# Two chained attention layers in 32-bit floats: layer 1's softmax without a maximum for seven of eight images, and a split load of the weights

## The chip, the core and the metric

The kernel runs on one core of a Trainium2 chip. The core has five engines that run side by side, each with its own queue of instructions: TensorE (PE, matrix products; PEld is its loading of the stationary operand), VectorE (DVE), ScalarE (ACT), GpSimd (POOL) and SyncE (SP), which in this kernel issues the DMAs. Matrix products are written to PSUM, which is used here in banks of 128 x 512 floats, and DVE and ACT carry them from there to SBUF. The metric is the device time of one execution in microseconds (us); lower is better.

## The reference

There are 8 images of 32 x 32 positions, so N = 1024 tokens, with C = 256 channels. Layer 0 is self-attention with 4 heads of width 256, an output projection and a residual. Layer 1 is a gated self-attention with keys of width 32. Cut to what matters:

```python
# layer 0
qkv = einsum('bnc,cd->bnd', x, W_qkv)            # 4 heads, q, k, v of 256 each
q, k, v = split(qkv.reshape(B, N, 4, 768), 3, axis=-1)
atten = softmax(einsum('bihd,bjhd->bijh', q, k) * 256 ** -0.5, axis=2)
res = einsum('bijh,bjhd->bihd', atten, v).reshape(B, N, 1024)
x = einsum('bnd,dc->bnc', res, W_out) + b_out + x
# layer 1
f, g, h = x @ Wf + bf, x @ Wg + bg, x @ Wh + bh  # widths 32, 32, 256
s = einsum('bik,bjk->bij', g, f)
o = einsum('bij,bjd->bid', softmax(s, axis=-1), h)
x = gamma * o + x
```

## The kernel before

**Layer 0** is cut into steps: one for each image, head and half of the queries (a block of 512). Weights are folded once at the start: `fold_weights(h)` turns the query, key and value weights of a head by PE (`pwq`, `pwk`, `pwv`, L293) and multiplies them to `wqk` and `wvo` (L309). After that a head needs the transposed image `x0T`, the products `q` of it with `wqk`, scores, exponentials, weighted sums `y` of the rows and a projection by `wvo` (`po`, L628), which is scaled by an inverse sum and added to the residual (L639). The three large products (queries, scores, weighted sums) are made from seven block products in place of eight. `seven` holds the recipe (its matmuls are L237, its additions L254), and DVE makes the sums of blocks that it needs: `sums` (L571) for the exponentials, `key_sums` (L396) for `x0T`, `value_sums` (L412) for the rows.

Layer 0's softmax takes no maximum. The sums of the exponentials go through DVE, an all-reduce on POOL (L584) and two small DMAs into columns, and their reciprocals are kept in `inverse` (L597). At the very end `judge` counts on DVE and POOL how many of the kept reciprocals lie within bounds, `decide` turns this into a flag, and if one does not, a branch runs everything again in a general form with maxima (`General0` and `Layer1`).

**Layer 1** of image b - 1 is a unit of two steps (`Layer1`). It stands between heads 1 and 2 of image b, for b = 7 behind the four heads; layer 1 of the last image (`final`) comes after all steps. `scores` makes eight products of 128 keys by 512 queries into eight PSUM banks (`ps_l`, L735), and ACT copies them to `s_l` (L744). `Softmax.have` takes maxima over the keys on DVE (L781, L785, L787) and over the partitions on POOL (L789). `pieces` subtracts the maximum on DVE (L796) and takes the exponential on ACT (L801), in four parts each. `row_products` then multiplies by the values, which carry a column of ones (`pa_l`, L814), takes the reciprocal of the sum (L822, into a small tile `r`) and adds the scaled product to the residual (L824).

**The order.** On PE, DVE and ACT the order is written out by hand: each step collects tasks with `put(tasks, *at)`, where `at` is a place within the step, and emits them sorted by place. An engine runs its queue in that order, so that an instruction that waits holds up all behind it. DMAs on SP and the work of POOL are placed by the framework. Six PSUM banks (`ps`) go round among scores, weighted sums and layer 1's products, and two others (`psm`) among the rest. A product that takes a bank waits until the bank's last reader is done.

The transposed image of the next image is made in two parts. 32 DMAs per image move blocks of 32 x 32 (`x0T<-x`, L368), and four DVE transposes (`squares`, L373) turn what lies within the blocks. The latter are placed at 0.4, 1.4, 2.4 and 4.4 of the step of head 3, block 0, of images 0 to 6.

**The start.** The first image is loaded, its blocks are transposed by PE (`px`, L341), and ACT copies them out (L344). `load_weights` issues two DMAs per head: all of its columns of `W_qkv` as one (L187) and its rows of `W_out` (L188). The biases and layer 1's weights follow (`load_rest`), then the next image.

Of the kernel before, what the change touches and what calls it, by code (L numbers as in the profile page):

```python
# [10 lines left out]
F32 = mybir.dt.float32  # L11
AF = mybir.ActivationFunctionType
# [8 lines left out]
def kernel(  # L21
# [63 lines left out]
    CV = C + 4  # L85
    SCALE = C ** (-0.5)
    SUM_LOW, SUM_HIGH = N / 8.0, N * 8.0


    x_v = x.rearrange("b h w c -> b (h w) c").rearrange("b (k p t) c -> b p k (t c)", p=P, t=HT)  # L90
# [60 lines left out]
    bh_sb = const.tile([P, C], F32, tag="bh", name="bh_sb")  # L151
    gamma_sb = const.tile([P, 1], F32, tag="gamma", name="gamma_sb")

    inverse = const.tile([P, B * HEADS * NBLK * HT], F32, tag="inverse", name="inverse")

    def load_rest():
# [24 lines left out]
    def load_weights(h, tag):  # L181

        nw = CC * 3 * C
        t = tile_of(tag, [P, nw + CC * C], f"w_{h}")
        w = t[:, :nw].rearrange("p (c d) -> p c d", c=CC)
        wo = t[:, nw:].rearrange("p (c d) -> p c d", c=CC)
        nc.sync.dma_start(w, wqkv_v[:, :, ts(h, 3 * C)])  # L187
        nc.sync.dma_start(wo, wout_v[:, ts(h, CC), :])  # L188
        weights[h] = w, wo

# [455 lines left out]
    class Layer1:  # L646
        scale = 1.0

        def __init__(self, b):
            self.b, self.name = b, f"{b}_l1"  # L650
            self.s = {}
            self.fg = None

# [71 lines left out]
        def scores(self, blk):  # L725

            n = f"{self.name}_{blk}"
            four = P // CK
            soft = Softmax(self, blk)

            def task(j0):
                pms = []
                for r in range(four):
                    pm = tile_of("ps", [P, NB], f"ps_{n}_{j0 + r}")
                    nc.tensor.matmul(  # L735
                        pm,
                        lhsT=self.f[ts(r, CK), ts(j0 + r, P)],
                        rhs=self.g[ts(r, CK), ts(blk, NB)],
                        start=True,
                        stop=True,  # L740
                    )
                    pms.append(pm)
                for r, pm in enumerate(pms):
                    nc.scalar.copy(soft.tile()[:, j0 + r, :], pm)  # L744

            have = [
                partial(soft.have, [(j0, j0 + 2), (j0 + 2, j0 + four)])
                for j0 in range(0, NT, four)
            ]
            return [partial(task, j0) for j0 in range(0, NT, four)], have + soft.pieces()  # L750

        def products(self, blk):
            return row_products(self, blk, rows1)
# [53 lines left out]
    def row_products(a, blk, acc_rows):  # L807


        def task(ti):  # L810
            p, v = a.s[blk], a.v
            pm = tile_of("ps", [P, NB], f"pa_{a.name}_{blk}_{ti}")
            for j in range(NT):
                nc.tensor.matmul(  # L814
                    pm[:, : C + 1],
                    lhsT=p[:, j, ts(ti, P)],
                    rhs=v[:, j, : C + 1],
                    start=(j == 0),
                    stop=(j == NT - 1),
                )  # L820
            r = tile_of("r", [P, 1], f"r_{a.name}_{blk}_{ti}")
            nc.vector.reciprocal(r, pm[:, C : C + 1])  # L822
            acc = acc_rows[a.b][:, blk * HT + ti, :]
            nc.vector.scalar_tensor_tensor(acc, pm[:, :C], r, acc, ALU.mult, ALU.add)  # L824
            a.done(blk, ti)

        return [partial(task, ti) for ti in range(HT)]
# [43 lines left out]
    for b in range(B):  # L871
        units = [Layer0(b, h) for h in range(HEADS)]
        if b > 0:
            units.insert(behind(b), Layer1(b - 1))
        steps += [(u, blk) for u in units for blk in range(NBLK)]
    final = Layer1(B - 1)

# [18 lines left out]
    for i, (a, blk) in enumerate(steps):  # L896
        l0 = isinstance(a, Layer0)
        one, two, nxt = step(i - 1), step(i - 2), step(i + 1)
        places = []

        def put(tasks, *at):
            assert len(tasks) == len(at)
            places.extend(zip(at, range(len(places), len(places) + len(at)), tasks))

        if l0:
            put(a.scores(blk), 0, 2, 4, 6, 8, 10)
        else:
            tasks, pieces = a.scores(blk)
            put(tasks, *((0.5, 2.4) if blk == 0 else (0.5, 2)))
            put(pieces, *((1.6, 3.9, 6.2, 6.5, 7.4, 8.4, 8.6) if blk == 0 else  # L910
                          (0.9, 2.7, 4.2, 5, 6.2, 6.8, 7.5)))
        if is_l0(two):
            u, k = two
            put(u.products_of[k][2:], 1 if l0 else 0)
            put([partial(u.invert, k)], 2.9 if l0 or blk == 1 else 1.9)
            put(u.project(k), *((3, 7) if l0 else (2, 6) if blk == 0 else (3, 7)))
        if is_l0(one):
            u, k = one
            sums, keys = u.sums(k)
            u.products_of[k] = u.products(k)  # L920
            put(sums[:2] + sums[3:], *((2.2, 3.2, 4.2) if l0 else (0.8, 2.2, 4.5)))
            put(sums[2:3], 5.2 if l0 else 5.5)
            put(keys, *((6.2, 8.2) if l0 else (7.6, 9.6)))
            put(u.products_of[k][:2], *((5, 9) if l0 else (4, 7)))
        elif one is not None:
            put(one[0].products(one[1]), *((3, 5, 7, 9) if l0 else (1, 4, 6, 8)))
        if i == 0:
            put(fold[2:], -2, -1, *[1.5 + 0.6 * n for n in range(len(fold) - 4)])
            put(first_sums[:2], 8.4, 9.4)
        if i == 1:  # L930
            put(first_sums[2:], 1.4, 3.4)
            put([partial(nc.vector.tensor_scalar, bh_sb, bh_sb, gamma_sb, None, ALU.mult)], 8.5)

        if is_l0(nxt) and blk == NBLK - 1:
            queries, qsums = nxt[0].queries()
            put(queries, *((2.5, 4.5, 6.5) if not l0 else
                            (1.5, 2.5, 4.5) if is_l0(two) else (0.5, 2.5, 5.5)))
            put(qsums, *((6.7, 6.9, 7.3, 7.6) if not l0 else
                          (5.4, 6.4, 7.2, 7.4) if is_l0(two) else (6.4, 7.2, 7.3, 7.4)))

        if l0 and a.h == 0 and blk == 0:
            put(residual(a.b), 5.3, 6.3, 7.3, 7.4)
        if l0 and a.h == 0 and blk == 1 and a.b > 0:
            put(value_sums(a.b), 1.4, 2.4, 3.4, 4.4)
        if l0 and a.h == 2 and blk == 0 and a.b + 1 < B:
            load_x(a.b + 1)
        if l0 and a.h == 2 and blk == 1 and a.b + 1 < B:
            moves, squares = turn_rows(a.b + 1, rows, xT_of, 0)
            put(moves, *range(1, 9))
        if l0 and a.h == HEADS - 1 and blk == 0 and a.b + 1 < B:  # L950
            put(squares, 0.4, 1.4, 2.4, 4.4)
            put(key_sums(a.b + 1), 5.4, 6.4, 7.2, 7.4)

        if l0 and a.b > 0 and a.h == behind(a.b) - 1:
            if blk == 0:
                moves, turned = turn_rows(a.b - 1, rows1, x1T_of, 1, step(i + 2)[0].fg_tile)
                put(moves, 0.1, 0.2, 0.3, 0.4)
                put(turned, 5.4, 6.4, 7.2, 7.4)
            else:
                tasks, moves = nxt[0].queries_apart()  # L960
                put(tasks, 1.5)
                put(moves, 1.6, 1.7, 1.8, 1.9)
        if not l0 and blk == 0:
            put(a.values(), 0.9, 1, 3, 5, 8)
        if nxt is None:
            put(transpose_rows(B - 1, rows1, x1T_of, 1), 8.1, 8.2, 8.3, 8.4)
            put(final.queries(), 9, 9.1, 9.3)
        for _, _, t in sorted(places, key=lambda x: x[:2]):
            t()


    count = const.tile([P, 1], F32, tag="count", name="count")
    total = const.tile([P, 1], F32, tag="total", name="total")
    flag = const.tile([P, 1], mybir.dt.int32, tag="flag", name="flag")

    def judge():
        n = inverse.shape[1]
        good = tile_of("rs", [P, n], "good")
        nc.vector.tensor_scalar(good, inverse, 1.0 / SUM_HIGH, None, ALU.is_ge)
        nc.vector.scalar_tensor_tensor(good, inverse, 1.0 / SUM_LOW, good, ALU.is_le, ALU.mult)  # L980
        nc.vector.tensor_reduce(count, good, op=ALU.add, axis=AX.X)
        nc.gpsimd.partition_all_reduce(total, count, P, bass_isa.ReduceOp.add)

    def decide():
        n = inverse.shape[1]
        nc.vector.tensor_scalar(flag, total, P * n - 0.5, None, ALU.is_lt)

    (s0, p0), (s1, p1) = final.scores(0), final.scores(1)
# [9 lines left out]
    class General0:  # L998
# [31 lines left out]
        def scores(self, blk):  # L1030
# [15 lines left out]

            return [partial(task, j0) for j0 in range(0, NT, 4)], soft.pieces()

        def done(self, blk, ti):
            pass  # L1050

# [54 lines left out]
```

## Time and profile before

| what | value |
|---|---|
| three runs: median (lowest to highest) | 2349.11 us (2348.98 to 2349.63) |
| the profiled execution: its time, its span | 2347.16 us, 2345.4 us |
| TensorE clock granted, mean | 1.000 |
| layer 1's subtraction, DVE L796 | 64 of 1217 ns |
| layer 1's maxima, DVE L781, L785, L787 | 32 of 1218, 16 of 1226, 16 of 692 ns |
| layer 1's exponential, ACT L801 | 64 of 1059 ns |
| layer 1's copy out of PSUM, ACT L744 | 128 of 600 ns |
| layer 1's maximum over partitions, POOL L789 | 16 of 1783 ns |

The page of the profile tells of one execution. The span runs from the first instruction to the last. Busy times count when at least one instruction of an engine is under way; on PE the ends of matmuls are modelled, and neighbours overlap. A line of the waits has the waiting engine, tile and line, what it waited for, and then the total in us, how often, and the longest. A line of the timeline has start, duration, engine, line, operation, output<-input, shapes and a count where equal instructions that follow each other are merged; a bracket at its end gives the idle time before it and what ended it. Line numbers are those of the kernel before.

### The profile page before, as it was taken

To read this page: it belongs to the slowest core of one execution; us is meant where nothing else is said; L and a number is where in the kernel's file an instruction comes from. 1 tells how busy PE (TensorE), PEld (TensorE's weight loads), DVE (VectorE), ACT (ScalarE), POOL (GpSimd) and SP (SyncE) were. 2 spreads that over 40 slices of the span, in tenths; PEclk is the share of its full clock that TensorE was granted. 3 is DMA by queue.
4 is the path that set the end of the run, shared out by engine and by line. 5 is a ranking of instruction groups with operands and counts; after the bars stand their busy time and mean duration, and the time that the engine had idled before them with its cause. 6 is when DMAs were issued, how large, how long until landed. Compare 5 with 4: busy or idle time off the path is not lost.

```text
span 2345.4 us, 26265 instructions
## 1 busy us (share of the span) xinstructions
PE 2329.4 (99%) x10394; PEld 1917.0 (82%) x10394; DVE 1606.1 (68%) x2506; ACT 580.0 (25%) x931; POOL 236.5 (10%) x93
## 2 busy tenths in 40 slices
PE   9999999999999999999999999999999999999999
PEld 6888888788878888788887888878888788888877
DVE  6667776577775767757777577675776757766665
ACT  2222222222232222322223222232222322222232
POOL 0111110011110111101111011110011101101110
PEclk9999999999999999999999999999999999999999
DMA  4000010100101001110011000110001100000100
GB/s 137 1 1 1 1 37 15 33 1 8 29 17 32 1 19 21 19 28 1 19 26 18 24 1 19 30 18 19 1 19 30 19 19 1 1 1 1 30 10 29
DMA packets 169172, 42.96 MB, mean 18 GB/s; under 512 B 158097, under 2 KB 161937, under 8 KB 169041
## 3 DMA queue, kind: packets, MB, share of 16 engines
q1 hardware_dynamic: 169040, 41.20, 7.9%
q8 instruction: 84, 1.38, 0.2%
q14 instruction: 48, 0.39, 0.1%
HBM read 13.37 MB, written 8.52 MB: 9 GB/s over the span
## 4 chain that ended last, share of the span: by engine, by line
PE 95%; DVE 4%; DMA 0%; ACT 0%; issue 0%; SPq 0%; DVEq 0%; ACTq 0%
PE psy L237 14%; PE psy_y L237 14%; PE psx L237 9%; PE pa_l L814 9%; PE psz L237 9%; PE po L628 9%; PE psx_y L237 9%; PE psz_y L237 9%; PE psy_q L237 4%; PE psx_q L237 2%; PE psz_q L237 2%; PE pr_v_l L457 2%; PE ps_l L735 1%; DVE s_l L796 1%; PE pm_fg L693 1%; DVE s L571 0%
## 5 line engine op out<-in xcount | busy, mean ns | idle before, releaser
L584 POOL PARTITION_ALL_REDUCE rb<-rs x64 | 206.9, 3233 | 1880.6 <-DVE rs L582 1880.6
L532 ACT ACTIVATE p<-p 128x1024 f32<-128x1024 f32 x128 | 135.3, 1057 | 562.1 <-DVE p L254 562.1
L237 PE MATMUL psx<-q,x0T 128*128 128x256 f32 x1024 | 263.5, 380 | 0.0
L237 PE MATMUL psy<-qs,xs 128*128 128x256 f32 x1024 | 262.9, 379 | 0.0
L237 PE MATMUL psz<-q,xs 128*128 128x256 f32 x1024 | 262.8, 379 | 0.0
L237 PE MATMUL psy_y<-s,xt 128*128 128x256 f32 x1024 | 243.0, 380 | 2.6 <-DVE s L571 2.4
L628 PE MATMUL po<-wvo,y 128*128 128x256 f32 x1024 | 242.0, 379 | 0.0
L237 PE MATMUL psx_y<-p,x 128*128 128x256 f32 x1024 | 241.9, 379 | 0.0
L814 PE MATMUL pa_l<-v_l,s_l 128*128 128x257 f32 x1024 | 231.7, 381 | 2.3 <-DVE y L254 1.9
L237 PEld LDWEIGHTS psx<-q,x0T 128*128 128x128 f32 x1024 | 193.9, 190 | 45.4 <-issue 20.7
L628 PEld LDWEIGHTS po<-wvo,y 128*128 128x128 f32 x1024 | 194.5, 190 | 40.0 <-issue 15.1
L814 PEld LDWEIGHTS pa_l<-v_l,s_l 128*128 128x128 f32 x1024 | 193.7, 190 | 39.0 <-issue 12.7
L237 PEld LDWEIGHTS psx_y<-p,x 128*128 128x128 f32 x1024 | 194.6, 190 | 34.1 <-issue 8.6
L237 PEld LDWEIGHTS psy_y<-s,xt 128*128 128x128 f32 x1024 | 191.6, 190 | 35.4 <-PE psx_y L237 5.0
L237 PEld LDWEIGHTS psy<-qs,xs 128*128 128x128 f32 x1024 | 194.5, 190 | 26.8 <-DVE qs L503 0.4
L237 PEld LDWEIGHTS psz<-q,xs 128*128 128x128 f32 x1024 | 194.6, 190 | 26.4
L254 DVE TENSOR_TENSOR u<-psy,e 128x512 f32<-128x512 f32 x128 | 88.5, 692 | 146.1 <-ACT e L260 73.5
L266 ACT ACTIVATE p<-psx 128x512 f32<-128x512 f32 x128 | 76.4, 597 | 409.8 <-PE psx L237 409.6
L254 DVE TENSOR_TENSOR v<-psy,e 128x512 f32<-128x512 f32 x128 | 88.0, 688 | 125.1 <-PE psy L237 125.1
L237 PE MATMUL psy<-qs,x0T 128*128 128x256 f32 x512 | 131.5, 379 | 0.8 <-DVE v L254 0.8
L639 DVE SCALAR_TENSOR_TENSOR x<-po,inverse,x 128x256 f32<-128x256 f32 x256 | 112.0, 479 | 16.9 <-PE po L628 6.6
L260 ACT COPY e<-psx 128x512 f32<-128x512 f32 x128 | 73.8, 577 | 201.4 <-PE psx L237 201.4
(116 smaller groups left out, 3056.7 us busy)
## 6 DMA issues: line engine op xcount, KB each, us to landing
out_dram<-x SPq DMA_DIRECT2D x15, 512.0 KB, 2.6
x<-in_x_dram SPq DMA_DIRECT2D x14, 512.0 KB, 4.8
x0T<-x SPq DMA_DIRECT2D x224, 32.0 KB, 1.9
fg<-x SPq DMA_DIRECT2D x112, 64.0 KB, 2.3
fg<-fg SPq DMA_DIRECT2D x56, 64.0 KB, 2.0
w<-in_L_conv_W_qkv_dram SPq DMA_DIRECT2D x4, 768.0 KB
x<-in_x_dram SPq DMA_DIRECT2D x4, 256.0 KB, 4.4
w<-in_L_conv_W_out_dram SPq DMA_DIRECT2D x4, 256.0 KB, 9.8
```

Of the source, the lines that this page charges most:

```text
L237: nc.tensor.matmul(banks[k][:, ts(i, w)], lhsT=lhsT, rhs=rhs, start=first and n == 0, stop=True, skip_group_check=True,)
L254: nc.vector.tensor_tensor(dst, shaped(banks[k]), shaped(other), ALU.add)
L260: nc.scalar.copy(scratch("e"), banks["x"])
L266: copy(outs["11"](), shaped(banks["x"]))
L457: nc.tensor.matmul(pm[:, ts(j, C)], lhsT=src()[:, c, ts(2 * t2 + j, P)], rhs=w()[:, c, :], start=(c == 0), stop=(c == CC - 1),)
L532: exp(both, both)
L584: nc.gpsimd.partition_all_reduce(t, r.rearrange("p e i -> p (e i)"), P, bass_isa.ReduceOp.add)
L628: nc.tensor.matmul(pm[:, ts(j, C)], lhsT=self.y[blk][:, c, ts(2 * t2 + j, P)], rhs=folded[self.h][1][:, c, :], start=(c == 0), stop=(c == ...
L639: nc.vector.scalar_tensor_tensor(acc, pm[:, ts(j, C)], inverse[:, n : n + 1], acc, ALU.mult, ALU.add)
L693: nc.tensor.matmul(pm[ts(k, half)], lhsT=w[:, c, :], rhs=x1T_of[b][:, c, ts(k, NB)], start=(c == 0), stop=(c == CC - 1),)
L735: nc.tensor.matmul(pm, lhsT=self.f[ts(r, CK), ts(j0 + r, P)], rhs=self.g[ts(r, CK), ts(blk, NB)], start=True, stop=True,)
L814: nc.tensor.matmul(pm[:, : C + 1], lhsT=p[:, j, ts(ti, P)], rhs=v[:, j, : C + 1], start=(j == 0), stop=(j == NT - 1),)
```

## The change

Four things are changed.

- For the first seven images, layer 1 takes the exponential directly when it carries the scores out of PSUM (`direct=True`). The maxima, their all-reduce, the subtraction and the later exponential are left out. The last image keeps them.
- The reciprocals of these images' sums are kept in a constant `inverse1` of 56 columns, and `judge` counts them too, within 2^-64 and 2^64, adding both counts.
- The third of the four transposes of `x0T` moves from place 2.4 to 3.4 of its step.
- `load_weights` splits the load of `W_qkv`: queries' and keys' columns first, then the values' columns.

```diff
         w = t[:, :nw].rearrange("p (c d) -> p c d", c=CC)
         wo = t[:, nw:].rearrange("p (c d) -> p c d", c=CC)
-        nc.sync.dma_start(w, wqkv_v[:, :, ts(h, 3 * C)])
+        for part in (slice(0, 2 * C), slice(2 * C, 3 * C)):
+            nc.sync.dma_start(w[:, :, part], wqkv_v[:, :, ts(h, 3 * C)][:, :, part])
         nc.sync.dma_start(wo, wout_v[:, ts(h, CC), :])
...
+            exp = partial(nc.scalar.activation, func=AF.Exp, scale=self.scale)
...
                 for r, pm in enumerate(pms):
-                    nc.scalar.copy(soft.tile()[:, j0 + r, :], pm)
-
+                    (exp if self.direct else nc.scalar.copy)(soft.tile()[:, j0 + r, :], pm)
+
+            tasks = [partial(task, j0) for j0 in range(0, NT, four)]
+            if self.direct:
+                return tasks, []
...
+        def inverse_of(self, blk, ti):
+            if self.direct:
+                n = (self.b * NBLK + blk) * HT + ti
+                return inverse1[:, n : n + 1]
+            return tile_of("r", [P, 1], f"r_{self.name}_{blk}_{ti}")
...
-            r = tile_of("r", [P, 1], f"r_{a.name}_{blk}_{ti}")
+            r = a.inverse_of(blk, ti)
...
-            units.insert(behind(b), Layer1(b - 1))
+            units.insert(behind(b), Layer1(b - 1, direct=True))
...
-            tasks, pieces = a.scores(blk)
+            tasks, _ = a.scores(blk)
             put(tasks, *((0.5, 2.4) if blk == 0 else (0.5, 2)))
-            put(pieces, *((1.6, 3.9, 6.2, 6.5, 7.4, 8.4, 8.6) if blk == 0 else
-                          (0.9, 2.7, 4.2, 5, 6.2, 6.8, 7.5)))
...
-            put(squares, 0.4, 1.4, 2.4, 4.4)
+            put(squares, 0.4, 1.4, 3.4, 4.4)
...
     def judge():
-        n = inverse.shape[1]
-        good = tile_of("rs", [P, n], "good")
-        nc.vector.tensor_scalar(good, inverse, 1.0 / SUM_HIGH, None, ALU.is_ge)
-        nc.vector.scalar_tensor_tensor(good, inverse, 1.0 / SUM_LOW, good, ALU.is_le, ALU.mult)
-        nc.vector.tensor_reduce(count, good, op=ALU.add, axis=AX.X)
+        for k, (inv, low, high) in enumerate(
+            ((inverse, SUM_LOW, SUM_HIGH), (inverse1, 1.0 / FAR, FAR))
+        ):
+            good = tile_of("rs", [P, inv.shape[1]], f"good{k}")
+            nc.vector.tensor_scalar(good, inv, 1.0 / high, None, ALU.is_ge)
+            nc.vector.scalar_tensor_tensor(good, inv, 1.0 / low, good, ALU.is_le, ALU.mult)
+            nc.vector.tensor_reduce(counts[:, k : k + 1], good, op=ALU.add, axis=AX.X)
+        nc.vector.tensor_tensor(count, counts[:, 0:1], counts[:, 1:2], ALU.add)
         nc.gpsimd.partition_all_reduce(total, count, P, bass_isa.ReduceOp.add)
```

More of the change, by code (lines that the diff above doesn't have):

```diff
@@ L87 @@
     SUM_LOW, SUM_HIGH = N / 8.0, N * 8.0
+    FAR = 2.0**64
     x_v = x.rearrange("b h w c -> b (h w) c").rearrange("b (k p t) c -> b p k (t c)", p=P, t=HT)
@@ L152 @@
     gamma_sb = const.tile([P, 1], F32, tag="gamma", name="gamma_sb")
+    inverse1 = const.tile([P, (B - 1) * NBLK * HT], F32, tag="inverse1", name="inverse1")
     inverse = const.tile([P, B * HEADS * NBLK * HT], F32, tag="inverse", name="inverse")
@@ L647, with __init__ @@
         scale = 1.0
-        def __init__(self, b):
-            self.b, self.name = b, f"{b}_l1"
+        def __init__(self, b, direct=False):
+            self.b, self.name, self.direct = b, f"{b}_l1", direct
             self.s = {}
@@ L749, in scores @@
             ]
-            return [partial(task, j0) for j0 in range(0, NT, four)], have + soft.pieces()
+            return tasks, have + soft.pieces()
+        def inverse_of(self, blk, ti):
[3 more added lines that the diff above has]
+            return tile_of("r", [P, 1], f"r_{self.name}_{blk}_{ti}")
         def products(self, blk):
@@ L972 @@
     count = const.tile([P, 1], F32, tag="count", name="count")
+    counts = const.tile([P, 2], F32, tag="counts", name="counts")
     total = const.tile([P, 1], F32, tag="total", name="total")
@@ L976, in judge @@
     def judge():
-        n = inverse.shape[1]
-        good = tile_of("rs", [P, n], "good")
-        nc.vector.tensor_scalar(good, inverse, 1.0 / SUM_HIGH, None, ALU.is_ge)
-        nc.vector.scalar_tensor_tensor(good, inverse, 1.0 / SUM_LOW, good, ALU.is_le, ALU.mult)
-        nc.vector.tensor_reduce(count, good, op=ALU.add, axis=AX.X)
+        for k, (inv, low, high) in enumerate(
[6 more added lines that the diff above has]
+        nc.vector.tensor_tensor(count, counts[:, 0:1], counts[:, 1:2], ALU.add)
         nc.gpsimd.partition_all_reduce(total, count, P, bass_isa.ReduceOp.add)
     def decide():
-        n = inverse.shape[1]
+        n = inverse.shape[1] + inverse1.shape[1]
         nc.vector.tensor_scalar(flag, total, P * n - 0.5, None, ALU.is_lt)
@@ L1047, in scores, with inverse_of @@
             return [partial(task, j0) for j0 in range(0, NT, 4)], soft.pieces()
+        def inverse_of(self, blk, ti):
+            return tile_of("r", [P, 1], f"r_{self.name}_{blk}_{ti}")
         def done(self, blk, ti):
```

## The prediction

> **What bounds the kernel now.** I read the page first, then the waits of TensorE (PE), then the timeline around each place where PE waits. From the page's head and its table of engines:
>
> ```profile
> span 2345.4 us, 26265 instructions
> ...
> PE 2329.4 (99%) x10394; PEld 1917.0 (82%) x10394; DVE 1606.1 (68%) x2506; ACT 580.0 (25%) x931; POOL 236.5 (10%) x93
> ```
>
> PE is the bound from end to end, and every other engine has a third of the span or more to spare. Work taken off DVE, ACT and POOL is worth only what it takes out of PE's waits. These are the waits of PE (total, times, longest) that bear on the change:
>
> ```profile
> PE psy_y L237 <- DVE s L571: 2.4, 7, 0.3
> PE pa_l L814 <- DVE y L254: 1.9, 7, 0.3
> PE pwq L293 <- DMA w<-in_L_conv_W_qkv_dram: 1.1, 1, 1.1
> ```
>
> They are few, and understated: matmuls overlap, so a wait counts as idle only once the one before has drained. I therefore measure from start to start. The timeline shows 8 matmuls of 256 columns in 1.89 us, with 0.38 us for one, so the pitch is (1.89 - 0.38) / 7 = 0.216 us. The first wait, in the period of image 2:
>
> ```profile
> 498.43 0.70 DVE L373 STREAM_TRANSPOSE x0T<-x0T 128x512 f32<-128x512 f32 x1
> 499.06 0.14 DVE L597 RECIPROCAL inverse<-st 128x4 f32<-128x4 f32 x1
> 499.21 1.89 PE L237 MATMUL psx_y<-p,x 128*128 128x256 f32 x8
> 499.30 0.88 DVE L639 SCALAR_TENSOR_TENSOR x<-po,inverse,x 128x256 f32<-128x256 f32 x2
> 500.09 1.22 DVE L571 TENSOR_TENSOR s<-ss,p 128x1024 f32<-128x1024 f32 x1
> 501.45 0.45 PE L237 MATMUL psy_y<-s,xt 128*128 128x256 f32 x1 [0.34 <-DVE s L571]
> ```
>
> `psy_y` was due at 499.21 + 8 x 0.216 = 500.94 and began at 501.45, 0.14 us after `s` was ready (500.09 + 1.22 = 501.31): 0.51 us lost. Its eight then took 1.97 us in place of 1.89, 0.08 more. So 0.58 us, once per image for images 0 to 6. Ahead of `s` stands one transpose that has no hurry.
>
> The second wait, in layer 1's second block:
>
> ```profile
> 407.62 1.22 DVE L796 TENSOR_TENSOR s_l<-s_l,cmax_l 128x1024 f32<-128x1024 f32 x1
> 408.75 0.69 DVE L581 TENSOR_TENSOR rs<-m 128x512 f32<-128x512 f32 x1
> 408.96 1.14 PE L735 MATMUL ps_l<-fg 32*128 32x512 f32 x8
> 409.81 0.42 DVE L254 TENSOR_TENSOR y<-psy_y,e_y 128x256 f32<-128x256 f32 x1
> 410.38 0.46 PE L814 MATMUL pa_l<-v_l,s_l 128*128 128x257 f32 x1 [0.27 <-DVE y L254]
> ```
>
> From the start of `ps_l` to the next work PE takes 1.42 us here. At the three other groups of `ps_l` in this layer (384, 389 and 414 us) it is 1.07. `pa_l` gets a PSUM bank that `y<-psy_y` empties, ready at 410.23, although PE had filled it by 407.4: DVE stood in the subtraction of the maximum. Loss 0.35 us, less 0.03 for the slower restart that the other groups show, so 0.32, again 7 times.
>
> **What the skill says.** "Perfetto Trace Analysis", Identifying the Most-Contended Engine, calls matmul busy time a poor measure because matmuls are pipelined. The trace agrees: weight loads fill 82% where PE shows 99%, and the 0.51 us above show as 0.34. "ScalarE: Activation LUTs", Step-by-step: what each stage is for, says that throughput is the same for every function. It agrees: exponentials out of PSUM (128x512) take 597 ns, layer 1's copies 600. "DMA: Bandwidth & Descriptors", Anatomy of one DMA (told there for GpSimd's path; these loads are SyncE's), says that the semaphore fires only after the last byte is confirmed. Here the last 3,072-byte packet of head 0's weights ends at 8.15 us and PE starts on them at 9.20. "TensorE: Matmul & The Clock Gate", Part 1: The HAM clock gate, says PE starts throttled until it has been busy for a while. It agrees: 128-column transposes have a pitch of 0.216 us up to 7.7 and 0.110 from 9.2.
>
> **The change, part by part.**
>
> *No maximum in 14 of layer 1's 16 blocks.* Per block it removes on DVE 2 x 1.218 + 1.226 + 0.692 + 4 x 1.217 = 9.2 us (rows L781, L785, L787, L796), on ACT 4 x 1.059 = 4.2 us (L801), on POOL 1.78 us (L789). Over 14 blocks that is 129, 59 and 25 us. The copy becomes an exponential, 600 against 597 ns: nothing, and banks come free as before. None of this is on the path but for the second wait. There the last subtraction ahead of `y<-psy_y` goes, and so do the three before it. DVE's `v_l`, `rs`, `rs` and `y` then follow their inputs, and `y<-psy_y` is done near 408, two microseconds before the bank is wanted at about 410.0. Gain 7 x 0.32 = 2.2 us. PE's own order is the same in both programs, instruction for instruction.
>
> *One transpose from 2.4 to 3.4.* DVE's order shows it directly behind `s`. The reciprocal and everything up to `s` move up by its 0.63 us (499.06 - 498.43): `s` ends at 500.68, PE may go at 500.82, and it is due at 500.94. The wait closes with 0.12 us to spare. The reciprocal's own input was issued at 492.05 and such a copy lands about 2 us later; `po` is there at 497.7. The transpose then ends at 501.3, where `p<-psy` (501.22) begins as before, and its reader, a key sum, starts at 505.61. Gain 7 x 0.58 = 4.1 us; without the restart 3.6.
>
> *Queries' and keys' weights first.* SP issues four more DMAs at about 0.45 us each; the bytes are the same. What queues behind them on SP are the biases, the next image's load (22.2 us) and its moves (29.4), whose product is first read near 200: hidden. Head 1's weights are wanted at 18.9 and their last packet ends at 10.75: hidden. Head 0's first two thirds arrive earlier: the 171st of 256 packets of 3,072 bytes ends at 7.05, so 1.1 us sooner. From the timeline of the start:
>
> ```profile
> 8.17 0.58 ACT L344 COPY x0T<-px 128x512 f32<-128x512 f32 x1 [0.27 <-PE px L341]
> ...
> 9.20 0.63 PE L293 MATMUL pwq<-ident,w 128*128 128x128 f32 x4 [1.07 <-DMA w<-in_L_conv_W_qkv_dram]
> 9.67 0.27 PE L293 MATMUL pwk<-ident,w 128*128 128x128 f32 x1
> ```
>
> `pwq` may then start near 8.1, at the slow pitch (4 x 0.216), and `pwk` near 8.9, since its bank is empty at 8.17 + 0.58 = 8.75. That is 0.8 us before 9.67. `pwv` newly waits for its own DMA, whose bytes were all there at about 9.1, and is due at about 9.8. All later waits of the start are chains between engines that move along. Bounds: 0 (the third copy gates) to 1.2 us; I take 0.8.
>
> *The judgement.* Three small DVE operations and one addition more. Nothing in the trace is this narrow and of this kind but reciprocals (166 ns); I bound them by 0.6 and 1.2 us in all (256-wide ones take 282 to 424 ns). DVE sat idle 0.99 us before the reciprocal that follows (at 2329.91), and PE waits for neither: nothing. Writing the reciprocals into a wider constant costs nothing.
>
> Sum: 4.1 + 2.2 + 0.8 = 7.1 us from a span of 2345.4. The runs' median is 2349.11, the profiled one's time 2347.16: launch and end lie outside the span and are not touched. 2349.1 - 7.1 = 2342.0, -0.30%. What a measurement of this kernel can tell from no change is about 0.2%, 4.7 us.
>
> **Rivals.** *The transposition closes nothing*, because `s` still comes a tenth late or another instruction takes the hole. For it: the margin is only 0.12 us. Against: even then most of 0.51 goes. Time: 2349.1 - 3.0 = 2346.1. *The bank wait stays*, with another holder of the bank: 2349.1 - 4.9 = 2344.2. Against it: DVE's end and PE's start are 0.15 us apart, as at the first wait. *The start gives nothing*: 2342.8, inside the forecast. *DVE's relief helps more than the two waits*: the remaining losses in the middle (0.18 us at `psy_y` once an image, changes between 32-row and full matmuls) lie where no removed instruction stands, so at most 7 x 0.26 = 1.8 more, 2340.2.
>
> *Slower: the judgement fails and the general path runs behind the fast one.* Place: the branch after the last product. It decides from a row sum outside 2^64 either way, 44.4 in logarithm. Price, estimated from the trace's pitches (256 columns 0.216, 512 columns 0.429, two passes each): a head needs 6.9 for queries, 6.9 for values, 27.5 for scores, 27.8 for products, so 276 us for four, and layer 1 some 35: 8 x 311 = 2490, in all 4835 us. Against it: worked out from the reference's inputs, the logarithms of layer 1's row sums lie between 10.9 and 33.6. Otherwise the change only takes work from queues whose order stays; the three things that it adds are the DMAs, the moved transpose and the judgement, all with slack above.
>
> **Chances.** Forecast (the start's rival with it) 0.76; bank wait stays 0.08, half of which still passes 0.2%; transposition closes nothing 0.12; more gain 0.02; slower 0.02. Faster 0.76 + 0.04 + 0.02 = 0.82, within 0.2% 0.04 + 0.12 = 0.16, slower 0.02. Range: low 2341.0 (all gains at their upper bound, 7.5, and the runs' spread of 0.6), high 2345.0, which takes in the bank rival and half closings of the first wait.
>
> **What would show it.** Right: both waits gone from PE's list, `s` ending 0.1 us or more before `psy_y` is due, 1.07 us from `ps_l` to `pa_l`, `pwk` near 8.9, DVE busy near 1477 us with PE's pitch unchanged. Wrong: a new releaser in front of `psy_y` or `pa_l`, PE waiting for a later weights copy, or a second pass over all images.

## The result, and the profile after

The changed kernel takes 2341.31 us (median of 6 runs, 2340.5 to 2343.82); the kernel before, beside it, 2349.05 (6 runs, 2347.45 to 2349.63). The ratio is 0.997, with an interval from 0.9957 to 0.9983: 4.0 to 10.1 us shorter. The forecast was 2342.0.

The head of the page of the changed kernel, its table of engines and the shares of the chain that ended last (line numbers in a view are those of its own kernel, from here on):

```profile
span 2341.0 us, 26029 instructions
...
PE 2329.5 (100%) x10394; PEld 1918.5 (82%) x10394; DVE 1482.5 (63%) x2398; ACT 522.8 (22%) x875; POOL 211.6 (9%) x79
...
PE 99%; DVE 1%; DMA 0%; ACT 0%; SPq 0%; issue 0%; ACTq 0%
```

PE does the same work in a span that is 4.4 us shorter. DVE lost 123.6 us of busy time, ACT 57.2 and POOL 24.9. The waits of PE in the changed kernel (total, times, longest):

```profile
PE px L344 <- DMA x<-in_x_dram: 1.9, 3, 1.4
PE pm_idle L873 <- DVE col L133: 1.1, 1, 1.1
PE psy L240 <- DVE v L257: 0.8, 1, 0.8
PE pwk L296 <- ACT wvo L176: 0.8, 1, 0.8
PE pwv L296 <- ACT wqT L176: 0.7, 1, 0.7
PE pa_l L828 <- DVE v_l L723: 0.4, 1, 0.4
```

Both lines with seven waits, `psy_y` for `s` and `pa_l` for `y`, are gone, and so is `pwq` for its DMA. What is left stands once or three times. The first line is in the start, where PE waits for the image, and it is longer than before:

```profile
PE px L341 <- DMA x<-in_x_dram: 0.6, 2, 0.4
```

I cut the span at two marks that every version has: the first matmul of the first `psy_y`, and the last matmul of the last `pa_l` (start to start, so that modelled ends play no part).

| | before | after | difference |
|---|---|---|---|
| start of the span to the first `psy_y` | 62.74 us | 64.66 us | +1.92 |
| first `psy_y` to the last `pa_l` ("the middle") | 2277.15 us | 2270.85 us | -6.30 |
| last `pa_l` to the end | 5.5 us | 5.5 us | 0 |

So the middle is 6.3 us shorter, and the start of this one execution is 1.9 us longer.

The timeline of the changed kernel in the period of image 2, where `psy_y` waited (start, duration, then what ran):

```profile
499.44 0.17 DVE L600 RECIPROCAL inverse<-st 128x4 f32<-128x4 f32 x1
499.72 0.88 DVE L642 SCALAR_TENSOR_TENSOR x<-po,inverse,x 128x256 f32<-128x256 f32 x2
500.23 1.89 PE L240 MATMUL psx_y<-p,x 128*128 128x256 f32 x8
500.51 1.22 DVE L574 TENSOR_TENSOR s<-ss,p 128x1024 f32<-128x1024 f32 x1
501.64 0.70 DVE L376 STREAM_TRANSPOSE x0T<-x0T 128x512 f32<-128x512 f32 x1
501.95 1.89 PE L240 MATMUL psy_y<-s,xt 128*128 128x256 f32 x8
```

The transpose now stands behind `s`. `psy_y` is due at 500.23 + 8 x 0.216 = 501.96 and starts at 501.95; all eight form one row of 1.89 us. `s` ends at 501.73, 0.22 us before; of that PE needs the usual 0.14 from DVE's end to its own start, so 0.08 us was to spare.

The place of the second wait in the changed kernel:

```profile
408.53 0.42 DVE L585 TENSOR_TENSOR rs<-rs 128x256 f32<-128x256 f32 x1
408.87 0.42 DVE L257 TENSOR_TENSOR y<-psy_y,e_y 128x256 f32<-128x256 f32 x1
410.29 1.14 PE L740 MATMUL ps_l<-fg 32*128 32x512 f32 x8
...
411.36 2.00 PE L828 MATMUL pa_l<-v_l,s_l 128*128 128x257 f32 x8
```

`y<-psy_y` has emptied the bank at 409.29. From `ps_l` to `pa_l` it is 411.36 - 410.29 = 1.07 us; before it was 1.42.

The start of the changed kernel:

```profile
4.75 2.05 PE L344 MATMUL px<-ident,x 128*128 128x128 f32 x8 [0.29 <-DMA x<-in_x_dram]
8.20 1.54 PE L344 MATMUL px<-ident,x 128*128 128x128 f32 x6 [1.40 <-DMA x<-in_x_dram]
9.61 1.08 PE L296 MATMUL pwq<-ident,w 128*128 128x128 f32 x4
10.49 1.06 PE L296 MATMUL pwk<-ident,w 128*128 128x128 f32 x4
...
12.39 2.53 PE L312 MATMUL pwqk<-wqT 128*128 128x256 f32 x8
```

In this view PE waits for the last part of the image, 1.40 us at 8.20, and `pwq` and `pwk` follow at once. But the weights were no earlier either. 16 DMA engines share a load, and each reports its part to the load's semaphore; the last of the sixteen records for the queries' and keys' columns comes at 9.47 us (9.07 for the one load before), and `pwq` starts 0.14 us behind it (0.13 before). The view shows no such wait, because the matmuls of the late image fill PE until then.

The four matmuls of `pwq` take 1.08 us; in the kernel before they took 0.63. PE has the full clock only from 13.7 us here, from 8.8 before: inside `pwqk` the pitch of 256 columns falls from 0.427 to 0.216 us at 13.7, so its eight take 2.53 us and not 1.89 as before.

The judgement in the changed kernel:

```profile
2323.89 0.19 DVE L994 TENSOR_SCALAR good<-inverse 128x56 f32<-128x56 f32 x1
2324.11 0.22 DVE L995 SCALAR_TENSOR_TENSOR good<-inverse,good 128x56 f32<-128x56 f32 x1
2324.36 0.21 DVE L996 TENSOR_REDUCE counts<-good 128x1 f32<-128x56 f32 x1
2324.61 0.16 DVE L997 TENSOR_TENSOR count<-counts 128x1 f32<-128x1 f32 x1
...
2325.29 0.15 DVE L1002 TENSOR_SCALAR flag<-total 128x1 int32<-128x1 f32 x1 [0.52 <-POOL total L998]
2325.52 0.17 DVE L836 RECIPROCAL r_l<-pa_l 128x1 f32<-128x1 f32 x1
```

The four new operations take 0.88 us from first start to last end. The reciprocal that follows the flag now starts right behind it, where DVE sat idle for 0.99 us before. PE has no wait there.

### The profile page after: what moved, and what is told of

Read it like the earlier page. It is cut to its first block, busy times and chain, and to the rows that moved or that the text cites. A ratio compares the mean times of both kernels' runs of the same rounds, so it can differ in the third digit from the quotient of the medians.

```text
span 2341.0 us, 26029 instructions
## 1 busy us (share of the span) xinstructions
PE 2329.5 (100%) x10394; PEld 1918.5 (82%) x10394; DVE 1482.5 (63%) x2398; ACT 522.8 (22%) x875; POOL 211.6 (9%) x79
## 4 chain that ended last, share of the span: by engine, by line
PE 99%; DVE 1%; DMA 0%; ACT 0%; SPq 0%; issue 0%; ACTq 0%
PE psy_y L240 14%; PE psy L240 14%; PE psx L240 10%; PE pa_l L828 9%; PE po L631 9%; PE psx_y L240 9%; PE psz_y L240 9%; PE psz L240 9%; PE psy_q L240 4%; PE psx_q L240 2%; PE psz_q L240 2%; PE pr_v_l L460 2%; PE ps_l L740 1%; PE pm_fg L697 1%; PE pwqk L312 0%; DMA x<-in_x_dram 0%
```

## The experiments

The theory that they test: the gain is the two waits, 4.1 and 2.2 us, each closed by what no longer stands ahead of one DVE instruction; the split load is worth little or nothing, and the start's 1.9 us belong to that execution. The rivals: the split itself holds up the image; the relief of DVE, not the order, makes the gain; the split is worth 0.8 us as forecast, and hidden by scatter.

The kernels ran in three sessions, each on one chip with its own runs of the kernel before. "Middle" and "first `psy_y`" are the two marks above, each from one profiled execution.

| kernel | runs | median, us | ratio to before | middle, us | first `psy_y`, us |
|---|---|---|---|---|---|
| before, session 1 / 2 / 3 | 46 / 22 / 9 | 2348.18 / 2348.46 / 2349.09 | 1 | 2277.15 | 62.74 |
| changed (first result) | 6 | 2341.31 | 0.9970 (0.9957 to 0.9983) | 2270.85 | 64.66 |
| 1 before_moved_transpose | 21 | 2343.89 | 0.9982 (0.9975 to 0.9988) | 2273.07 | 64.02 |
| 1 before_direct | 13 | 2346.07 | 0.9993 (0.9985 to 1.0001) | 2274.94 | 66.12 |
| 1 before_split_load | 13 | 2347.44 | 0.9999 (0.9991 to 1.0007) | 2277.14 | 62.72 |
| 1 after_one_load | 10 | 2342.36 | 0.9976 (0.9967 to 0.9986) | 2270.85 | 65.23 |
| 2 order_only | 9 | 2342.21 | 0.9974 (0.9964 to 0.9984) | 2270.85 | 63.90 |
| 2 after_queries_last | 13 | 2343.38 | 0.9978 (0.9970 to 0.9987) | 2270.85 | 64.98 |
| 2 after_sums_early | 6 | 2340.18 | 0.9966 (0.9953 to 0.9978) | 2269.57 | 62.36 |
| 2 sums_early_idle9 | 5 | 2339.53 | 0.9961 (0.9947 to 0.9975) | 2269.57 | 62.63 |
| 3 idle9_one_load | 5 | 2338.82 | 0.9957 (0.9943 to 0.9971) | 2269.22 | 61.94 |
| 3 idle9_split (the same kernel as sums_early_idle9) | 5 | 2339.09 | 0.9959 (0.9945 to 0.9973) | 2269.57 | 61.39 |
| 3 idle9_order_only | 5 | 2338.74 | 0.9957 (0.9944 to 0.9971) | 2269.22 | 61.99 |

The middle is the sharp measure, although each is one execution. Every start of PE in it agrees to 0.01 us between two executions of one program (sums_early_idle9 and idle9_split), and between versions that differ only in the load, with one exception of 0.35 us that is told below. So what one part does can be read to a hundredth of a microsecond, where the medians scatter by one or two.

### One part alone

*The transpose alone*, on the kernel before:

```diff
-            put(squares, 0.4, 1.4, 2.4, 4.4)
+            put(squares, 0.4, 1.4, 3.4, 4.4)
```

> The kernel before with nothing but the third transpose moved from 2.4 to 3.4. My theory: the wait of psy_y for s closes, 7 x 0.58 = 4.1 us, about 2345.0. Rival (another instruction takes the hole): under 1 us.

The middle is 2273.07, 4.08 us less than before. PE's waits in this kernel have lost the line of `psy_y`; the other one stands as it was:

```profile
PE pa_l L814 <- DVE y L254: 1.9, 7, 0.3
```

*The direct exponentials alone*, with the wider judgement, which they need; transpose and load as before:

```diff
-                    nc.scalar.copy(soft.tile()[:, j0 + r, :], pm)
+                    (exp if self.direct else nc.scalar.copy)(soft.tile()[:, j0 + r, :], pm)
...
-            units.insert(behind(b), Layer1(b - 1))
+            units.insert(behind(b), Layer1(b - 1, direct=True))
```

> The kernel before with nothing but the direct exponentials and the wider judgement. My theory: only the bank wait goes, 7 x 0.32 = 2.2 us, about 2346.9, although DVE loses 129 us of work. Rival (DVE's relief helps elsewhere too, the wait of psy_y for s among it): 4 us or more.

The middle is 2274.94, 2.21 us less than before. Here the other line is gone, and in PE's waits this one stays, unchanged, although DVE has 129 us less to do:

```profile
PE psy_y L239 <- DVE s L573: 2.4, 7, 0.3
```

The two parts do not touch each other: 4.08 + 2.21 = 6.29, and together they made 6.30. Set beside those of before, PE's starts shift at seven places for each part, 0.51 + 0.08 us at each `psy_y` and about 0.32 at each `pa_l`, and nowhere else by more than 0.05. The median of this run fell by 2.1 us, which by itself can't be told from no change; the middle can.

*The split load alone*, on the kernel before:

```diff
-        nc.sync.dma_start(w, wqkv_v[:, :, ts(h, 3 * C)])
+        for part in (slice(0, 2 * C), slice(2 * C, 3 * C)):
+            nc.sync.dma_start(w[:, :, part], wqkv_v[:, :, ts(h, 3 * C)][:, :, part])
```

> The kernel before with nothing but the split load. My theory: 0.8 us faster, about 2348.3. Rival (the split holds up the first image): 0 to 2 us slower, 2349 to 2351, with PE waiting for x in the profile.

The ratio is 0.9999 (0.9991 to 1.0007), and even in the profile nothing moved: `pwq` starts at 9.18 us (9.20 before) and still waits for its DMA, in PE's waits of this kernel:

```profile
PE pwq L294 <- DMA w<-in_L_conv_W_qkv_dram: 0.9, 1, 0.9
```

The records of this load's semaphore tell why. Fifteen of the sixteen engines had reported the queries' and keys' columns by 7.95 us, half a microsecond earlier than with one load (8.45). The last one came at 9.04; with one load, at 9.07. The wait ends with the last. "DMA: Bandwidth & Descriptors", Why a DMA increments its semaphore by 16 and not by 1, describes this: the engines finish independently, each adds one to the semaphore behind its own data, and only all 16 mean that everything has landed. The records agree; that the last stands 1.1 us behind the fifteenth is this run's figure.

*The change without the split*: the changed kernel with one load per head again (the diff above the other way round).

> The changed kernel with W_qkv of a head loaded by one DMA again. My theory (two waits in the middle are worth 6.3 us, the split load 0.8 us at the start): 6.3 us faster than before, about 2342.8. Rival, from the profile of the changed kernel, where PE stood 1.4 us for the first image's load: the split's extra DMAs hold up the image, and without them the kernel is 1 to 2 us faster than the changed one, about 2340.5.

2342.36 us, its interval overlapping that of the changed kernel. In its profile too PE waits for the image (twice, 1.1 us the longer) and the first `psy_y` starts at 65.23, later than with the split. So a late image needs no split. Over all 13 profiles its last part has landed between 6.24 and 8.31 us with one load (six of them) and between 6.24 and 8.16 with the split (seven); that rival falls. The late image of the changed kernel's profile is within the scatter of the start.

### Order or amount of work

*The order alone.* All maxima, subtractions and exponentials of before stay. The transposition is moved, and of the three DVE instructions that stood between PE's filling of the bank and `y<-psy_y` (a subtraction and the two additions `rs`, L581 and L582, of the sums of exponentials) the two sums go behind `y`, into the next step:

```diff
-            put(keys, *((6.2, 8.2) if l0 else (7.6, 9.6)))
+            if l0:
+                put(keys, 6.2, 8.2)
+            elif blk == 0:
+                put(keys[:1], 7.6)
+                late = keys[1:]
+            else:
+                put(keys, 7.6, 9.6)
...
+            if late:
+                put(late, 0.2)
+                late = []
...
-            put(squares, 0.4, 1.4, 2.4, 4.4)
+            put(squares, 0.4, 1.4, 3.4, 4.4)
```

> The kernel before, with every maximum, subtraction and late exponential kept and one load per head. Only DVE's order is changed: the third transpose at 3.4, and the last two additions of the sums of head 1, block 1 (L581, L582, 1.06 us in the queue) put behind the two y of layer 1's second block. My theory (the change pays by what stands ahead of two instructions on DVE, not by the work it removes): both waits close, 6.3 us faster than before, about 2341.9, and from the first psy_y to the last pa_l 2270.9 us as in the changed kernel (2277.2 before). Rival (the removed 129 us of DVE work matter in themselves): only the transposition's 4.1 us, 2273.1 in the middle.

The head of its page:

```profile
span 2340.1 us, 26265 instructions
...
PE 2329.1 (100%) x10394; PEld 1918.4 (82%) x10394; DVE 1609.7 (69%) x2506; ACT 581.2 (25%) x931; POOL 236.6 (10%) x93
```

and its timeline at the second wait's place:

```profile
408.19 1.22 DVE L796 TENSOR_TENSOR s_l<-s_l,cmax_l 128x1024 f32<-128x1024 f32 x1
409.32 0.42 DVE L254 TENSOR_TENSOR y<-psy_y,e_y 128x256 f32<-128x256 f32 x1
409.53 1.14 PE L735 MATMUL ps_l<-fg 32*128 32x512 f32 x8
...
409.99 0.68 DVE L581 TENSOR_TENSOR rs<-m 128x512 f32<-128x512 f32 x1
410.60 2.65 PE L814 MATMUL pa_l<-v_l,s_l 128*128 128x257 f32 x11
```

DVE works as long as before (1609.7 us) and the subtraction still stands ahead of `y`. But `y` is done at 409.74, and `pa_l` starts 410.60 - 409.53 = 1.07 us behind `ps_l`. The middle is 2270.85 us, equal to the changed kernel's to the hundredth, and the median is 2342.21. Each of the 10,140 matmuls recorded from the first `psy_y` on starts within 0.011 us of its place in the changed kernel. Removing 129 us of DVE work, 59 of ACT and 25 of POOL brought what moving three instructions brings.

### The start

*Queries' and keys' weights last*: in the changed kernel each head loads its rows of `W_out` first, then the values' columns, then queries' and keys'.

```diff
-        for part in (slice(0, 2 * C), slice(2 * C, 3 * C)):
-            nc.sync.dma_start(w[:, :, part], wqkv_v[:, :, ts(h, 3 * C)][:, :, part])
         nc.sync.dma_start(wo, wout_v[:, ts(h, CC), :])
+        for part in (slice(2 * C, 3 * C), slice(0, 2 * C)):
+            nc.sync.dma_start(w[:, :, part], wqkv_v[:, :, ts(h, 3 * C)][:, :, part])
```

> The changed kernel with the three loads of each head in the opposite order: output weights, values' columns, queries' and keys' columns last. If bytes ahead in the queue set when PE can start on head 0's weights, 0.5 MB more stand ahead of them, at about 390 KB per us 1.3 us: 1.3 us slower than the changed kernel, about 2342.6, and pwq waiting for the DMA by that much more. Rival (single late packets and the clock's grant set the start): within 0.5 us of the changed kernel.

From its timeline:

```profile
9.76 0.63 PE L296 MATMUL pwq<-ident,w 128*128 128x128 f32 x4 [2.00 <-DMA w<-in_L_conv_W_qkv_dram]
```

The image was in time here and PE waited 2.00 us for the queries' columns, whose last engine reported at 9.62. The median is 2343.38; against the changed kernel's 2341.31 that is later by about 2 us, where 1.3 was expected, but the two come from different sessions and their intervals overlap. The kernel order_only, of the same session and with the same middle, is 1.2 us faster, with intervals that overlap too. So the order of the loads may cost something; that does not mean that the split earns it.

*The sums earlier.* The forecast had left 0.18 us (0.26 with the restart) at `psy_y` once an image as a loss that nothing removed could touch. It stands in the second step of head 2 (of image 0: head 0), and the same remedy fits: one addition of `sums` goes from place 3.2 of its step to 2.4.

```diff
-            put(sums[:2] + sums[3:], *((2.2, 3.2, 4.2) if l0 else (0.8, 2.2, 4.5)))
+            early = l0 and is_l0(nxt) and blk == NBLK - 1 and not is_l0(two)
+            put(sums[:2] + sums[3:], *((2.2, 2.4, 4.2) if early else
+                                       (2.2, 3.2, 4.2) if l0 else (0.8, 2.2, 4.5)))
```

> The changed kernel, with the second sum of a block placed at 2.4 in place of 3.2 in the seven steps where psy_y still waits 0.18 us for it, so that it stands ahead of v_q and q on DVE. My theory: this wait closes too, 7 x 0.26 = 1.8 us, about 2339.5, 2269.0 us from the first psy_y to the last pa_l. Rival (v_q and q, now 1.2 us later, hold up PE's next queries): no gain or a loss of some tenths per step.

The middle falls to 2269.57, by 1.28 us. Image 0's loss lies ahead of the first mark, so 6 x 0.26 = 1.6 was to be seen; one single wait of 0.34 us, new at 651.8, takes the rest. There DVE stands idle before an instruction that elsewhere follows the reciprocal at once:

```profile
649.65 0.88 DVE L642 SCALAR_TENSOR_TENSOR x<-po,inverse,x 128x256 f32<-128x256 f32 x2 [0.46 <-DVE inverse L600]
```

The reciprocal that the view names had ended 0.46 us before; what DVE waited for is open. This wait is also in sums_early_idle9 and idle9_split, but not in the two other kernels with the early sums, whose middle is 2269.22. One of these, idle9_one_load, differs from idle9_split in the load alone.

*More matmuls before the image arrives.* `pm_idle` (L873) runs idle products at the very start. Nine in place of five, with the early sums:

```diff
-    for _ in range(5):
+    for _ in range(9):
```

> As the one with the early sum, with 9 in place of 5 idle matmuls ahead of the first image, so that PE is busy from 1.05 to 4.9 us. They stand 0.5 us or less in the way of px. If the spread of the start comes from the clock, which was granted at 8.2 to 15.8 us in the profiles so far, it comes at 8 us more often: 0.5 to 1 us faster in the median than without. Rival (late packets of the image set the start): 0 to 0.5 us slower.

2339.53 us, 0.65 below the version with five. Five runs lie within 1.1 us, against 2.1 for that version's six, too few to call the difference shown. The full clock comes at 5.2 us. In this and the next three kernels it came between 5.2 and 6.9, with five idle products between 4.4 and 15.8 (once it was taken back). "TensorE: Matmul & The Clock Gate", Part 1: The HAM clock gate, says that PE starts throttled and that activity releases it; these profiles agree, though the 4.4 shows that five products can be enough.

*The load again, in a steadier start.* Three kernels with nine idle products and early sums: with one load, with the split, and the order-only kernel with all maxima (and the split).

> The kernel with the early sum and 9 idle matmuls, whose start spreads least, with W_qkv of a head loaded by one DMA again. My theory (the split is worth 0.8 us): 0.8 us slower than the same with the split, about 2340.3. Rival (the last of the 16 engines' packets to land decides, and it comes no earlier with the split): the same within 0.3 us.

> The kernel with the early sum and 9 idle matmuls, as run before, here beside the other two on one chip: about 2339.5.

> The same start and split load and the same three changes of DVE's order, but every maximum, subtraction and late exponential kept, and the sums of head 1, block 1 behind y. My theory (the removed work is worth nothing once the order is mended): the same as with it removed within 0.5 us, and 2269.6 us from the first psy_y to the last pa_l. Rival (with DVE that full, the early sum holds up other work): slower by 1 us or more.

With one load (its timeline) and with the split (its timeline), `pwq` starts so:

```profile
8.58 0.63 PE L295 MATMUL pwq<-ident,w 128*128 128x128 f32 x4 [0.51 <-DMA w<-in_L_conv_W_qkv_dram]
```

```profile
7.38 1.07 ACT L347 COPY x0T<-px 128x512 f32<-128x512 f32 x2 [0.26 <-PE px L344]
8.02 0.66 PE L296 MATMUL pwq<-ident,w 128*128 128x128 f32 x4 [0.19 <-ACT x0T L347]
```

Here the load works as meant: `pwq` is 0.56 us earlier and waits only for ACT, which copies the image out of the bank. In the times it is not to be seen: 2339.09 with the split, 2338.82 without. In both single profiles the first `psy_y` follows `pwq` (61.39 and 61.94), so half a microsecond may be there in a start that goes well. But the version with the split has the wait of 0.35 us in its middle (2269.57 against 2269.22), and that takes most of it back. The runs do not resolve the rest.

The third has the lowest median of the study, level with the two beside it: 2338.74, with every maximum still computed. Order changes, the split and four more idle products give 10.35 us against before (2349.09), 0.9957 (0.9944 to 0.9971). That beats before clearly; it is also 2.6 us below the changed kernel, across sessions and with intervals that overlap; 1.6 of these are the middle (2270.85 - 2269.22).

## Why the prediction was right, and where it was not

*PE is the bound, and removed work elsewhere counts only through PE's waits:* right, and shown by order_only.

*The transpose, 7 x 0.58 = 4.1 us with a margin of 0.12:* right. It measured 4.08 alone; the margin was 0.08. So the restart of 0.08 us per wait belongs into the sum: 7 x 0.51 would have been 3.6.

*The bank wait, 7 x 0.32 = 2.2 us:* right. It measured 2.21 alone. `y<-psy_y` ends at 409.29 where `ps_l` begins 1.33 us later than before; on before's scale that is 407.96, against "near 408". The forecast spoke of the last subtraction and the three before it. order_only shows that this is more than was needed: taking the two `rs`, 1.1 us, out from ahead of `y` does it.

*The general path does not run, the judgement is hidden:* right; 0.88 us lie within the 0.6 to 1.2. DVE's busy time is 1482.5 and not 1477: a fall of 123.6 for 129 us of removed rows. Busy time is a union and neighbours overlap, so rows of mean durations add up to more than they occupy. On ACT it is 57 for 59; on POOL, where nothing overlaps, 25 for 25.

*The other rivals:* neither wait stayed and no other releaser took its place, and the middle fell by 6.30 with 6.29 explained, so DVE's relief added nothing beyond the two waits.

*The split load, 0.8 us:* this step failed. It read "Head 0's first two thirds arrive earlier: the 171st of 256 packets of 3,072 bytes ends at 7.05, so 1.1 us sooner", and put `pwk` near 8.9. In the changed kernel's profile `pwk` starts at 10.49. Two things were wrong in it.

The packets were counted in the order of their ends, as if they formed one queue; they are spread over 16 engines, each with its share of every load, and a load ends with the slowest of them. The packet read as the last of head 0's weights ends at 8.15, but the last of the sixteen records comes at 9.07. In 11 of the 13 profiles, with the split and without, `pwq` starts 0.13 to 0.14 us behind the last record of the load that it needs; in the two others, both with the split, the image's matmuls and copies ended later still. That record comes between 8.45 and 10.30 us in six profiles with one load (9.23 on average) and between 7.83 and 9.47 in six with the split in the order of the change (8.68). So the split may bring it half a microsecond forward, not 1.1, under a scatter of more than one; in the pair of before and before_split_load it brought 0.03.

And the step took the rest of the start as fixed, while late loads and the clock that PE is granted move it by more than the effect: in the profiles with five idle products the first `psy_y` starts anywhere from 62.36 to 66.12 us. The 1.92 us that the changed kernel's profile lost are 0.41 by which `pwq` started later, with its last record, and 1.51 from there to the first `psy_y` (55.05 us, 53.54 before), where PE ran at half speed up to 13.7 us. That stretch took 53.34 to 53.54 us in the six profiles whose full clock came before `pwq`, and 54.71 to 55.69 in the five in which it came between 12.6 and 15.8. (The slow pitch of 128 columns is 0.213 us by the starts, not 0.216; nothing hangs on it.)

The sum that the runs support is therefore 4.08 + 2.21 + 0 = 6.3 us, 2342.8, the rival "the start gives nothing" inside the forecast. The medians' 7.7 us agree with it and with 7.1 alike (4.0 to 10.1). That the measured time came within 0.7 us of 2342.0 is in part luck, and no support for the 0.8. Of the 6.3 us, 4.1 come from the moved transpose, which the title does not name. Against the spans' 4.4: before's profile had a good start and the changed kernel's a poor one, which is why neither difference of spans should be read as the gain.

What remains open: how much of the split shows in the long run. The profiles point to half a microsecond or less, but the interval of before_split_load alone reaches from 2.1 us faster to 1.6 slower, and no run here tells nothing from a half. Why one of 16 engines lags, what sets the time of the full clock, and what causes the wait at 651.8 were not tried.

## What to carry to other kernels

On the bounding engine, list the waits, measure each from start to start, and ask what stands ahead of its releaser on that releaser's in-order queue; moving it cost nothing here and was worth as much as removing 129 us of work. Cut the span at marks that both versions have before comparing profiles: here the middle of one program repeats to 0.01 us where runs scatter by two. What an earlier load is worth was set by its last engine, not by the mean of its packets: look for the last record, also where the list of waits does not name the load.

## What the runs showed of the hardware that was not expected

- A load's last engine can lag far behind the other fifteen: 9.04 us against 7.95 for the queries' and keys' columns in before_split_load. Over the 13 profiles this lag, for the load that `pwq` needs, is anything from 0.01 to 1.17 us.
- The full clock of PE came at 4.4 us in after_queries_last, was taken back at 11.3, after the wait of 2.00 us, for 3.4 us, and was full again from 14.7. Over the other profiles with five idle products it came between 8.2 and 15.8.
- DVE operations of the judgement on 1 to 56 columns take 153 to 216 ns: the same operation (TENSOR_SCALAR) takes 153 on one column and 191 on 56.
